# A state-space mixer: a block's weighted values move behind the whole gate, and the next transposes follow them

## The chip, the cores and the metric

The kernel runs on one core of a Trainium2 chip. The metric is the device time of one execution in microseconds (us), and a kernel's time is the median of its runs. Five engines matter here, each with its own queue of instructions that it works through in order: TensorE (PE; its weight loads are shown as PEld), VectorE (DVE), ScalarE (ACT), GpSimd (POOL) and SyncE (SP, which here only issues DMA transfers). Engines wait for each other on semaphores. An instruction that waits holds up everything behind it in its own queue.

## What is computed

The reference is one layer of a hybrid model over x of 4 x 256 tokens with 512 channels, in float32, four residual steps one after the other: attention, a feed-forward step with a choice of clusters, a state-space mixer, and the same feed-forward step again.

```python
x = x + attn(layernorm(x))
x = x + ffn(layernorm(x))
x = x + mixer(layernorm(x))     # the part that the change touches
x = x + ffn(layernorm(x))
```

The mixer projects 512 channels to a gate (8192), values (8192), B and C (1024 each) and a step dt (128), sends values, B and C through a causal convolution of four taps and SiLU, and then for each of 128 heads of 64 values:

```python
scores  = einsum('bcihn,bcjhn->bcijh', Cc, Bc) * Ldec * dt      # Ldec = exp(cum_i - cum_j), lower triangle
y_intra = einsum('bcijh,bcjhp->bcihp', scores, xc)
y       = y_intra + y_inter + D * x        # y_inter: the state carried over chunks of 32
g       = y * silu(gate)
out     = (g * rsqrt(mean(g*g per group of 1024) + eps) * norm_w) @ out_w.T
```

The kernel folds the carried state into the scores: for each head it holds the decay between pairs of 64-token pieces of a sequence of 256, so y is one weighted sum.

## The kernel before

The attention and the first feed-forward step take the first 22% of the time or so. The mixer then runs over 64 blocks of 128 channels, two heads each, and is what this document is about. Eight blocks form a group (g is the group, gi the block's place in it, 0 to 7), which shares one B and C and one normalization.

A block i, `block()` at L1514, has these pieces. The names are those of the tiles in the profile.

- **x**: the projection of its 128 value channels for all 1024 tokens, 24 matmuls of 128 x 512 (L115 to L117) in two halves of 12, into a PSUM tile `pp`. Each product is made of three matmuls on split operands. There are two `pp` buffers, and the projections of x, gate, B and C go through them in turn.
- **conv and taps**: ScalarE copies x with scale and bias (`acc`, L963), VectorE adds three taps (L973). ScalarE applies SiLU and writes the tile `x` (L1145), which needs a table load because the block also uses exp.
- **gate**: 24 more matmuls into the other `pp`, and SiLU on ScalarE into `gt` (L1436).
- **decays**: for two heads, VectorE subtracts cumulative steps (`em`, L1194 and L1195, `differences`), ScalarE takes exponentials (L1206 to L1214, `exponentials`, which begin with the exp table load), VectorE multiplies by the scores `gm` (L1219, `weighted`). There are three `em` buffers and two are used by a block. The differences are made at the end of block i, the exponentials and the product with `gm` in block i+1.
- **transposes**: `turned()` (L1221) sends x through eight 128 x 128 transposes on TensorE (`trx`, L1226) into two PSUM tiles, and VectorE multiplies both by dt into `xd` (L1229). There is one `xd` buffer.
- **weighted values**: `product()` (L1237) makes 64 small matmuls of `em` and `xd` into the PSUM tile `pyy` (L1245).
- **gating**: `gated()` (L1252) adds D times x (L1257, two instructions) and multiplies by `gt` (L1260) into `gb` on VectorE. `spilled()` (L1263) writes `gb` of block i-2 to DRAM. That DMA is issued from ScalarE's queue at the very start of block i, ahead of the block's exponentials. `squared()` (L1270) sums the squares on ScalarE and POOL.
- **output product**: at gi >= 2, and at gi = 0 from group 2 on, 24 matmuls (`pog`) for an eighth of an earlier group's output stand between x and gate. At gi = 1 the output product (`first_out`) stands after the gate instead, behind a sum of squares over the finished group (`pqs`, L1315), and `trq` (L1327) follows it. The first group has no output product. Its operands (`gh`, `wo`) are split into two parts on ScalarE (L1352, L1299) and VectorE (L1357, L1302), and so are the weights `w` (L910, L913).
- **B and C** of the next group are projected at the end of blocks gi = 3 and 4 and go through their own taps in the following block. Their scores (`pg`, L1163, `gm`, L1170) are made in block gi = 6; in group 0 the second half waits for block 7.

The tiles `tr`, `trx`, `pg`, `pog`, `pqs` and `trq` share one PSUM pool of two buffers (tag "m"), in the order in which they are made.

The order of the instructions on TensorE, VectorE, ScalarE and POOL is written out by hand in the mixer: they stand as the Python calls come. The values of block i-1 are thus finished in block i. Before the change, TensorE's order in a block with an output product is: first half of x(i), transposes of x(i-1), second half of x(i), output product, weighted values of i-1, gate(i). Without an output product between them it is: x(i) with the transposes of x(i-1) in its middle, gate(i), weighted values of i-1. `last_block()` (L1665) replaces the end of block 63.

Of the kernel before, what the change touches and what calls it, by code (L numbers as in the profile page):

```python
# [79 lines left out]
def hybrid_kernel(  # L80
# [789 lines left out]
    def mixer(feed, ps, mnorm, later):  # L870
        with ExitStack() as es, ExitStack() as inner:
# [32 lines left out]
            def upper_piece(i):  # L904

                if i >= NW:
                    return lambda: None
                w = pieces[i] = [pw.tile([P, KC, P], F32R, name=f"w{j}", tag=f"w{j}") for j in range(2)]
                r = raws.pop(i)
                nc.scalar.copy(w[0], r)  # L910

                def lower():
                    nc.vector.tensor_tensor(w[1], r, w[0].bitcast(F32), ALU.subtract)  # L913
                    fetch(i + 3)

                return lower
# [201 lines left out]
            def piece(v, j, c, k=0, n=None):  # L1118

                at, step = 4 * c + j * 7 + k * (1 + 2 * j), 1 + 2 * j  # L1120
                n = 4 - c - k if n is None else n
                return v[:, at : at + (n - 1) * step + 1 : step, :]
# [62 lines left out]
            def own_and_next(e):  # L1185
                return pieces_of(e, 0, 4, 4, 7), pieces_of(e, 1, 8, 2, 9)

            def differences(h):

                e = p2.tile([P, 20, Q], F32, name="em", tag="em", bufs=3)  # L1190
                own, next_ = own_and_next(e)
                rv = rr[h].rearrange("p (j c i) -> p j c i", j=2, c=4)
                cv = col_t[:, :, h : h + 1].rearrange("p (j c) h -> p j c h", j=2)
                nc.vector.tensor_tensor(own, rv, cv.to_broadcast([P, 2, 4, Q]), ALU.subtract)  # L1194
                nc.vector.tensor_tensor(  # L1195
                    next_, rv[:, :, 1::2, :], cv[:, :, 0::2].to_broadcast([P, 2, 2, Q]), ALU.subtract
                )
                return e
# [22 lines left out]
            def turned(n, x2):  # L1221

                xd = p2.tile([P, TT, P], F32, name="xd", tag="xd", bufs=1)
                trs = [ps.tile([P, 4, P], F32, name="trx", tag="m") for _ in range(2)]
                for c in range(TT):
                    nc.tensor.transpose(trs[c // 4][:, c % 4, :], x2[:, c * P : (c + 1) * P], ident)  # L1226
                for half, tr in enumerate(trs):
                    hs = slice(half * 4, half * 4 + 4)
                    nc.vector.tensor_tensor(  # L1229
                        xd[:, hs, :].rearrange("p c (h d) -> p c h d", h=2),  # L1230
                        tr.rearrange("p c (h d) -> p c h d", h=2),
                        dt_t[:, hs, 2 * n : 2 * n + 2].unsqueeze(3).to_broadcast([P, 4, 2, PD]),
                        ALU.mult,
                    )
                return xd

            def product(xd, es2):  # L1237
                py = ps_y.tile([P, 2, 2 * L], F32, name="pyy", tag="pyy")
                for j in range(2):
                    for c in range(4):  # L1240
                        for u in range(2):
                            us = slice(u * Q, (u + 1) * Q)
                            for hh in range(2):
                                d = slice(hh * PD, (hh + 1) * PD)
                                nc.tensor.matmul(  # L1245
                                    py[d, u, j * L + c * Q : (j + 1) * L].rearrange("p (k i) -> p k i", i=Q),
                                    xd[us, 4 * j + c, d], piece(es2[hh], j, c)[us],
                                    start=(c == 0), stop=(c == 3),
                                )
                return py  # L1250

            def gated(n, x2, gt, py):  # L1252

                gb = po_.tile([P, NT], F32, name="gb", tag="gb", bufs=3)
                for u, h in enumerate(hs):
                    k = lambda v: v.rearrange("p (k i) -> p k i", i=Q)
                    nc.vector.scalar_tensor_tensor(  # L1257
                        k(gb[:, h]), pair(x2)[:, :, u], dh[:, n : n + 1], k(py[:, u]), ALU.mult, ALU.add
                    )
                nc.vector.tensor_tensor(gb, gb, gt, ALU.mult)  # L1260
                return gb
# [124 lines left out]
            def projected(kind, n):  # L1386

                w = pieces.pop(at[kind, n])
                pp = (
                    ps_y.tile([P, NT], F32, name="pp", tag="pyy") if (kind, n) == ("g", 0)  # L1390
                    else ps_p.tile([P, NT], F32, name="pp", tag="pp")
                )
                for half in range(2):
                    yield pp
                    project(w, pp, slice(half * 512, half * 512 + 512))
                yield pp
# [27 lines left out]
            def outer(q, t):  # L1424

                po = ps.tile([P, C], F32, name="pog", tag="m")
                for half in range(2):
                    partial(po, q, parted.pop((q, 2 * t + half)), half)
                return q, t, po

            xs2, gts, ems, xds, gbs = {}, {}, {}, {}, {}
# [10 lines left out]
            def turn(i):  # L1442
                xds[i] = turned(i, xs2[i])
# [5 lines left out]
            def inner_products(i):  # L1449
                finish(i, product(xds.pop(i), ems.pop(i)))  # L1450

            def finish(i, py):
                gbs[i] = gated(i, xs2[i], gts.pop(i), py)
# [60 lines left out]
            def block(i):  # L1514
# [8 lines left out]
                def lowered():  # L1523
                    for f in lower:
                        f()
                    lower.clear()
# [20 lines left out]
                pp = next(x_steps)  # L1547
                waiting = [k for k in "bc" if k + "pp" in group]

                def begun_next(k):  # L1550
                    group[k] = conv(group[k + "pp"], (NB if k == "b" else NB + G) + g + 1, False)
# [11 lines left out]
                decays(i - 1, (0,) if between else (0, 1))  # L1563
                for k in waiting if g else ():
                    begun_next(k)
                turn(i - 1)
                if between:
                    weighted(ems[i - 1][0], gms[(i - 1) // GB])
                else:
# [14 lines left out]
                done = outer(*out) if out and not first_out else None  # L1584
# [6 lines left out]
                g_steps = projected("g", i)  # L1591
# [7 lines left out]
                both = i == NB - 1  # L1599
                scoring = None  # L1600

                def scored():
                    nonlocal scoring
                    if gi == 6 and g + 1 < G:
                        scoring = scores(group.pop("b"), group.pop("c"))
                        gms[g + 1] = next(scoring)
                        next(scoring)
                        next(scoring)

                next(g_steps)  # L1610
                for _ in pending:
                    for _ in pending.pop():
                        pass
                if done and not both:
                    inner_products(i - 1)
                    pp = next(g_steps)
                    scored()
                    next(g_steps)
                else:
                    pp = next(g_steps)  # L1620
                    next(g_steps)
                    scored()
                    if both:
                        return last_block(i, pp)
                    inner_products(i - 1)
                lower.append(upper_piece(n + 3))
                if g and gi == 0:
                    lower.append(upper_half(g - 1, 0))
# [1 line left out]
                if g and gi == 1:  # L1630
                    lower.append(upper_half(g - 1, 2))
                ems[i] = [differences(h) for h in (2 * i, 2 * i + 1)]
                lowered()
                if scoring and g:
                    for _ in scoring:
# [29 lines left out]
            def last_block(i, pp):  # L1665

                g = i // GB
                py = product(xds.pop(i - 1), ems.pop(i - 1))
                done = outer(G - 2, TT - 1)
                for k in range(3):  # L1670
                    fetch_out(NB - 3 + k)
                ems[i] = [differences(h) for h in (2 * i, 2 * i + 1)]
                made(0, 0)()
                gate(i, pp)
                decays(i, (0,))
                lower = [upper_out(g * GB + k) for k in range(4)]
                lower.append(made(1, 0))
                for f in lower[:2]:
                    f()
                scaled(*done)  # L1680
                for f in lower[2:]:
                    f()
                weighted(ems[i][0], gms[g])
                finish(i - 1, py)
                decays(i, (1,))
                made(2, 0)()
                turn(i)
                weighted(ems[i][1], gms[g])
                spilled(i - 1, gbs[i - 1])

            opening()
            for i in range(2, NB):
                block(i)
            es_p.close()
            ps_o = pool("m_o", 4, space=PSUM, **freed)
            i = NB - 1
# [208 lines left out]
```

## Time and profile before

| | |
|---|---|
| median of 3 runs | 1828.85 us (1825.78 to 1831.57) |
| the profiled execution, its own time | 1827.35 us |
| its span | 1825.5 us |
| mean granted clock of TensorE | 0.992 of full speed |
| PE busy | 1766.7 us |
| DVE busy | 1431.6 us |
| ACT busy | 1281.0 us |
| POOL busy | 249.8 us |
| a plain block of the mixer (start of pyy to start of pyy) | 19.8 us |
| a group of eight blocks | 173.1 us |

How to read the lines that follow. In a timeline a line gives the start (us from the span's start), the length, the engine, the line of the kernel, the operation, out<-in with sizes, the number of instructions merged, and in brackets the engine's idle time before it with what ended it. In the list of waits a line gives who waited for whom: us in total, times, the longest. In a table by stretches a line gives the stretch, its length, the busy time of PE, PEld, DVE, ACT and POOL (with instructions), the granted clock of TensorE, the DMA share and GB/s. In the page's first part a line gives the busy time of each engine with its share of the span. The chain is the work that ended last, followed back through what released each step.

### The profile page before, as it was taken

To read this page: it belongs to the slowest core of one execution; us is meant where nothing else is said; L and a number is where in the kernel's file an instruction comes from. 1 tells how busy PE (TensorE), PEld (TensorE's weight loads), DVE (VectorE), ACT (ScalarE), POOL (GpSimd) and SP (SyncE) were. 2 spreads that over 40 slices of the span, in tenths; PEclk is the share of its full clock that TensorE was granted. 3 is DMA by queue.
4 is the path that set the end of the run, shared out by engine and by line. 5 is a ranking of instruction groups with operands and counts; after the bars stand their busy time and mean duration, and the time that the engine had idled before them with its cause. 6 is when DMAs were issued, how large, how long until landed. Compare 5 with 4: busy or idle time off the path is not lost.

```text
span 1825.5 us, 33067 instructions
## 1 busy us (share of the span) xinstructions
PE 1766.7 (97%) x12862; PEld 1437.8 (79%) x12862; DVE 1431.6 (78%) x2163; ACT 1281.0 (70%) x2545; POOL 249.8 (14%) x255
## 2 busy tenths in 40 slices
PE   8999989899999999999999999999999999999998
PEld 6777767677877888888888888888888888888877
DVE  6566667788998788878878787879787878887777
ACT  6666676378788667766776686668667866777754
POOL 6322230010110111011101110010111011101100
PEclk9999999999999999999999999999999999999999
DMA  4000000212325323432442353325232533343231
GB/s 148 1 1 1 23 15 1 58 56 86 108 97 167 105 93 116 123 103 93 142 131 81 105 156 99 99 87 161 92 106 89 167 105 92 115 134 116 83 97 59
DMA packets 134381, 169.45 MB, mean 93 GB/s; under 512 B 12240, under 2 KB 77648, under 8 KB 134224
## 3 DMA queue, kind: packets, MB, share of 16 engines
q1 hardware_dynamic: 125152, 134.30, 24.5%
q10 hardware_dynamic: 9072, 33.03, 4.8%
q8 instruction: 101, 1.65, 0.4%
q14 instruction: 56, 0.46, 0.1%
HBM read 131.64 MB, written 35.65 MB: 92 GB/s over the span
## 4 chain that ended last, share of the span: by engine, by line
PE 81%; DVE 9%; ACT 6%; issue 2%; POOL 1%; DMA 1%; SPq 0%; ACTq 0%; DVEq 0%; POOLq 0%
PE pp L115 13%; PE pp L117 13%; PE pp L116 13%; PE pyy L1245 7%; PE pog L115 6%; PE pog L117 6%; PE pog L116 6%; PE trx L1226 3%; ACT e L504 2%; DVE acc L973 1%; PE pq L115 1%; PE ptr L520 1%; PE pq L116 1%; PE pq L117 1%; PE pg L1163 1%
## 5 line engine op out<-in xcount | busy, mean ns | idle before, releaser
L115 PE MATMUL pp<-mx,w 128*128 128x512 f32 x1144 | 459.6, 402 | 0.0
L117 PE MATMUL pp<-mx,w 128*128 128x512 f32 x1144 | 447.1, 391 | 0.0
L116 PE MATMUL pp<-mx,w 128*128 128x512 f32 x1144 | 446.5, 390 | 0.0
L1278 POOL TENSOR_TENSOR sq<-sq,x 128x1024 f32<-128x1024 f32 x54 | 132.1, 2447 | 1177.8 <-ACT x L1277 1177.8
L117 PEld LDWEIGHTS pp<-mx,w 128*128 128x128 f32 x1144 | 214.8, 188 | 46.0
L115 PEld LDWEIGHTS pp<-mx,w 128*128 128x128 f32 x1144 | 215.0, 188 | 44.6
L973 DVE SCALAR_TENSOR_TENSOR acc<-pp,cw_s,acc 128x1012 f32<-128x1012 f32 (+2 forms) x192 | 244.6, 1274 | 4.3
L116 PEld LDWEIGHTS pp<-mx,w 128*128 128x128 f32 x1144 | 215.3, 188 | 40.4
L1219 DVE TENSOR_TENSOR em<-em,gm 128x1280 f32<-128x1280 f32 x128 | 189.6, 1489 | 72.1 <-ACT em L1214 72.0
L115 PE MATMUL pog<-wo,gh 128*128 128x512 f32 x512 | 201.3, 393 | 1.9 <-DVE x L1374 1.9
L117 PE MATMUL pog<-wo,gh 128*128 128x512 f32 x512 | 200.3, 391 | 0.9 <-DVE gh L1357 0.9
L116 PE MATMUL pog<-wo,gh 128*128 128x512 f32 x512 | 200.0, 391 | 0.0
L1229 DVE TENSOR_TENSOR xd<-trx,dt_t 128x512 f32<-128x512 f32 x128 | 82.4, 686 | 141.4 <-PE trx L1226 141.4
L1145 ACT ACT_TABLE_LOAD x63 | 80.8, 1283 | 138.8 <-DVE acc L973 138.7
L1436 ACT ACTIVATE gt<-pp 128x1024 f32<-128x1024 f32 x64 | 65.7, 1026 | 145.3 <-PE pp L117 145.3
L1245 PEld LDWEIGHTS pyy<-em,xd 64*64 64x64 f32 x4096 | 130.3, 133 | 44.1 <-issue 17.3
L1206 ACT ACTIVATE em<-r,end_t 128x128 f32<-128x128 f32 x512 | 163.0, 389 | 0.8
L1245 PE MATMUL pyy<-em,xd 64*64 64x256 f32 (+3 forms) x4096 | 157.8, 300 | 3.1 <-DVE em L1219 2.9
L504 ACT ACTIVATE e<-sc,nmx 128x256 f32<-128x256 f32 (+1 forms) x256 | 104.0, 441 | 21.0 <-DVE nmx L498 20.9
L115 PEld LDWEIGHTS pog<-wo,gh 128*128 128x128 f32 x512 | 96.3, 188 | 24.7 <-issue 2.7
L117 PEld LDWEIGHTS pog<-wo,gh 128*128 128x128 f32 x512 | 96.4, 188 | 22.3 <-DVE gh L1357 2.1
L116 PEld LDWEIGHTS pog<-wo,gh 128*128 128x128 f32 x512 | 96.5, 188 | 19.4
(327 smaller groups left out, 3191.9 us busy)
## 6 DMA issues: line engine op xcount, KB each, us to landing
wr<-in_win_dram SPq DMA_DIRECT2D x144, 256.0 KB, 2.7
r<-cumd SPq DMA_DIRECT2D x256, 128.0 KB, 2.9
spill<-gb ACTq DMA_DIRECT2D x63, 512.0 KB, 2.8
gr<-spill SPq DMA_DIRECT2D x120, 256.0 KB, 3.4
wor<-in_wout_dram SPq DMA_DIRECT2D x64, 256.0 KB, 4.7
out_dram<-x SPq DMA_DIRECT2D x7, 256.0 KB, 2.9
x<-in_x_dram SPq DMA_DIRECT2D x1, 1536.0 KB, 8.8
gr<-spill SPq DMA_DIRECT2D x8, 192.0 KB, 2.5
```

The source lines that it names most:

```text
L115: nc.tensor.matmul(o, lh, rh, start=(first and k == 0), stop=False)
L116: nc.tensor.matmul(o, lh, rl, start=False, stop=False)
L117: nc.tensor.matmul(o, ll, rh, start=False, stop=(last and k == n - 1))
L504: nc.scalar.activation(es_[c][:, 2 * j + pr, :], sc[:, j, :], AF.Exp, bias=nm[:, j : j + 1], accum_out=rs[:, c, h : h + 1],)
L973: nc.vector.scalar_tensor_tensor(av[:, :, d:], pv[:, :, : L - d], cw_s[:, ch, tap : tap + 1], av[:, :, d:], ALU.mult, ALU.add,)
L1145: nc.scalar.activation(pair(x2).rearrange("p k u i -> p u k i"), acc.rearrange("p (u k i) -> p u k i", u=2, i=Q), AF.Silu,)
L1206: nc.scalar.activation(piece(e, j, c, 2 - c, 2), rv[:, j, 2:, :], AF.Exp, bias=end_t[:, 2 * j + c, h : h + 1],)
L1219: nc.vector.tensor_tensor(e, e, gm, ALU.mult)
L1229: nc.vector.tensor_tensor(xd[:, hs, :].rearrange("p c (h d) -> p c h d", h=2), tr.rearrange("p c (h d) -> p c h d", h=2), dt_t[:, hs, 2 * ...
L1245: nc.tensor.matmul(py[d, u, j * L + c * Q : (j + 1) * L].rearrange("p (k i) -> p k i", i=Q), xd[us, 4 * j + c, d], piece(es2[hh], j, c)[us ...
L1278: (nc.gpsimd if n < NB - 2 else nc.vector).tensor_tensor(sqs[g], sqs[g], x2, ALU.add)
L1436: nc.scalar.activation(gts[i], pp, AF.Silu)
```

## The change

No instruction is added or removed. In every block from 2 on:

- the weighted values of block i-1 always go behind both halves of gate(i), as they did before only where there was no output product;
- the transposes of x(i), with their two VectorE products, are issued in block i itself, directly behind these weighted values, instead of in the middle of x(i+1) in the next block. Block 2 still turns x(1) at the old place, since the opening does not;
- the gating of block i-1 (`finish`) is issued after those transposes. On VectorE the order at the end of a block becomes: `em` differences of i, `xd` of i, `gb` of i-1, then the subtractions that were collected in `lower`. Before it was `gb`, `em`, the subtractions, and `xd` in the next block.

On SP and POOL the order stays the same. On ScalarE too the instructions keep their order.

```diff
@@ block(i), between the two halves of x(i) @@
                 decays(i - 1, (0,) if between else (0, 1))
                 for k in waiting if g else ():
                     begun_next(k)
-                turn(i - 1)
+                if i == 2:
+                    turn(i - 1)
                 if between:
                     weighted(ems[i - 1][0], gms[(i - 1) // GB])
                 else:
@@ block(i), from the gate on @@
-                if done and not both:
-                    inner_products(i - 1)
-                    pp = next(g_steps)
-                    scored()
-                    next(g_steps)
-                else:
-                    pp = next(g_steps)
-                    next(g_steps)
-                    scored()
-                    if both:
-                        return last_block(i, pp)
-                    inner_products(i - 1)
+                pp = next(g_steps)
+                next(g_steps)
+                scored()
+                if both:
+                    return last_block(i, pp)
+                py = product(xds.pop(i - 1), ems.pop(i - 1))
                 lower.append(upper_piece(n + 3))
                 ...
                 ems[i] = [differences(h) for h in (2 * i, 2 * i + 1)]
+                turn(i)
+                finish(i - 1, py)
                 lowered()
```

`inner_products(i)` was `finish(i, product(...))`, so `product` and `finish` are the same calls as before, now apart.

## The prediction

> **What bounds the kernel now.** I read the page's busy shares and chain first, then the waits, then the timelines of single blocks.
>
> ```profile
> PE 1766.7 (97%) x12862; PEld 1437.8 (79%) x12862; DVE 1431.6 (78%) x2163; ACT 1281.0 (70%) x2545; POOL 249.8 (14%) x255
> ...
> PE 81%; DVE 9%; ACT 6%; issue 2%; POOL 1%; DMA 1%; SPq 0%; ACTq 0%; DVEq 0%; POOLq 0%
> ```
>
> TensorE is the bound. The list of waits shows how far behind it the others are:
>
> ```profile
> ACT gt L1436 <- PE pp L117: 145.3, 47, 5.2
> DVE xd L1229 <- PE trx L1226: 141.4, 48, 6.3
> ACT L1145 <- DVE acc L973: 138.7, 54, 4.9
> DVE em L1219 <- ACT em L1214: 72.0, 83, 1.2
> ```
>
> VectorE waits about 3 us a block for the transposes, ScalarE 3 us for the gate: that is all the slack there is. One plain block (gi=0) on ScalarE, then on VectorE; its transposes started at 1048.40:
>
> ```profile
> 1045.94 0.33 ACTq L1266 DMA_DIRECT2D spill<-gb  x1
> 1046.91 1.28 ACT L1206 ACT_TABLE_LOAD   x1
> 1060.35 1.06 ACT L1145 ACTIVATE x<-acc 128x1024 f32<-128x1024 f32 x1
> ...
> 1049.04 1.29 DVE L1229 TENSOR_TENSOR xd<-trx,dt_t 128x512 f32<-128x512 f32 x2 [3.57 <-PE trx L1226]
> 1055.08 3.89 DVE L973 SCALAR_TENSOR_TENSOR acc<-pp,cw_s,acc 128x1012 f32<-128x1012 f32 x3
> 1060.15 1.40 DVE L1257 SCALAR_TENSOR_TENSOR gb<-x,dh,pyy 128x512 f32<-128x512 f32 x2
> ```
>
> The new x is ready at 1061.41, 14.50 after the exp table load; today nobody asks for it until the next block. The second block of a group (gi=1), which has no output product between x and gate, on TensorE, VectorE, ScalarE:
>
> ```profile
> 1077.34 2.41 PE L1245 MATMUL pyy<-em,xd 64*64 64x256 f32 x64
> 1079.68 0.64 PE L1315 MATMUL pqs<-sq,ones 128*32 128x256 f32 x8
> ...
> 1079.89 2.73 DVE L1302 SCALAR_TENSOR_TENSOR wo<-wor,nw_s,wo 128x512 fp32r<-128x512 f32 x4
> 1082.54 1.40 DVE L1257 SCALAR_TENSOR_TENSOR gb<-x,dh,pyy 128x512 f32<-128x512 f32 x2
> ...
> 1080.66 1.06 ACT L1145 ACTIVATE x<-acc 128x1024 f32<-128x1024 f32 x1
> ```
>
> Here x ends at 1081.72, 2 us after pyy has left TensorE, and VectorE is late too. Two waits that will matter exist already, in the first group and in the last block:
>
> ```profile
> 441.74 0.33 ACTq L1266 DMA_DIRECT2D spill<-gb  x1
> 442.15 1.28 ACT L1206 ACT_TABLE_LOAD   x1 [1.91 <-DVE gb L1260]
> ...
> 1724.25 0.69 DVE L1194 TENSOR_TENSOR em<-r,col_t 128x512 f32<-128x512 f32 x1 [3.67 <-PE pyy L1245]
> ```
>
> The spill sits on ScalarE's queue ahead of the exponentials, so they wait for gb. The second em tile of a block waits for pyy of the block before, since there are three em buffers.
>
> **The change: what is removed.** No instruction. Per block 64 pyy matmuls move behind 24 gate matmuls, and 8 transposes (L1226) plus their 2 VectorE products xd (L1229) move from inside the next x to directly behind pyy, ahead of gb. None of them issues a DMA. The order on SP and POOL stays; only the spill's issue on ScalarE is met later, because its gb is later. Going back from float32 to the projection's matmuls costs 0.10 (1017.34 to 1017.67, against 0.227 a matmul). pyy and trx now share one return: between 0 and 0.2 a block saved; I take 0.1, as measured for one return. A plain block has 19.78 now (pyy at 1098.16 and 1117.94), so TensorE would need 19.68: 16.31 for 72 matmuls, 2.44 for pyy with the 0.10 of lead-in that it shows (1014.68 to 1015.00), 0.89 for the transposes and the return (1048.40 on), and 0.04 of small gaps.
>
> **What is added: a loop.** Call T the start of a block's transposes, X that of xd. pyy ends 0.07 after T, em's second tile starts 0.08 later and takes 0.94 (1724.25 to 1725.19): X = T+1.09. xd 1.21 (1029.24 to 1030.45), gb 2.66 (1060.15 to 1062.81), then 0.43 to the table load: X+4.30. x follows at +14.50, with 0.05 for the signal: the next T is at least T + 1.09 + 4.30 + 14.50 + 0.05 = T+19.9. Before, the load followed the gate 1.5 us before the transposes; now it comes 5.4 behind them. VectorE closes a loop of its own, since xd stands behind the scaled output, the weight and gh subtractions and em: 4.30 + 11.98 (load to end of taps, 1058.89) + 2.46 (1119.22 to 1121.68) + 1.87 (1104.34 to 1106.21) = 20.6. What is queued behind the waiting spill is all of a block's exponentials, then the copy that opens the taps; behind the waiting xd it is gb, and so the spill again. Both loops are longer than 19.68.
>
> **Group by group**, with gi the block's place in its group of eight (a group takes 173.1 us now, pyy at 1015.06 and 1188.18):
> - gi=3 and gi=0: 19.9 each instead of 19.8, +0.3 together. In gi=3 VectorE's loop is the longer (20.6 from X to X, where T moves 18.85 from X), so it ends 1.8 behind: X = T+1.8.
> - gi=4: the 5.44 us b projection gives the x loop room, but VectorE's b taps end at X + 4.30 + 8.17 (load to taps, 1055.08) + 3.82 (three taps, 461.04 to 464.86), 18.1 after T, and the gate wants their PSUM buffer at 0.89 + 16.31 = 17.2 (0.89 is the transposes with their return): a stall of 0.9, less 0.1 saved: +0.8. gi=5, with X = T+1.1 again: +0.1.
> - gi=6 and 7: scores and transposes share two PSUM buffers. VectorE does the first gm products (0.92) and em (1.87) before xd, so X = T+1.4. The third score tile waits for half of xd (0.69), at T+2.1 instead of T+0.9, the fourth for the rest; x starts at T+3.45. T to T: 21.3 in gi=6 (0.89 + 16.31 + two score tiles with a wait for the scaled output, 1.65, + 2.44), 3.45 + 16.31 + 2.44 = 22.2 in gi=7, together 43.5 against 42.6: +0.9.
> - gi=1: TensorE reaches the transposes at 0.89 + 10.88 + 2.44 = 14.2 after T of gi=0. x is ready at 1.09 + 4.30 + 15.01 (load 1066.71, x 1081.72; ScalarE's wo copies delay it by 0.5) = 20.4. VectorE then has wo and em to finish: X = 1.09 + 4.30 + 15.83 (to 1082.54) + 1.87 = 23.1. pqs and pog need the two PSUM buffers that xd frees, so pog starts at 24.5 instead of 15.6, a stall of 8.9. gi=1 and gi=2 together: 48.9 against 40.5 (pyy at 1057.62 and 1098.16): +8.4. In gi=2 ScalarE's chain has 3 us to spare, so TensorE does not get it back and does not lose more.
> - The clock, once a group behind gi=1's stall. The nearest row is the stall at 1754, with the clock in the third column from the right:
>
> ```profile
> 1754.00:1756.00 2.00, 0.07 (x2) 0.07 (x1) 1.86 (x5) 0.10 (x1) 0.00 (x0) 1.00 0.56 168
> 1756.00:1758.00 2.00, 2.00 (x8) 1.58 (x9) 1.57 (x6) 0.90 (x3) 0.00 (x0) 0.83 0.77 258
> 1758.00:1760.00 2.00, 2.00 (x6) 1.46 (x5) 1.93 (x5) 0.00 (x0) 0.00 (x0) 0.50 0.06 17
> ```
>
> TensorE idled 1.93; from 1757.19 to 1760.05 seven matmuls took 2.86 where 1.59 is usual, the transposes behind them 0.3 too long: 1.6 lost. Bounds: 0 (if gi=1's transposes keep it awake) and 3.2 (two dips); I take 1.6, the row itself.
>
> The Trainium skill, "TensorE: Matmul & The Clock Gate", Part 1, says that the clock halves after an idle window of about 3.4 us and needs about 3.4 us of work to return. That speaks against this change: it would price a dip at 1.7, in all 7 x 1.7 = 12 where the row gives 7 x 1.6 = 11. The row shows that a shorter idle can do it.
>
> A group thus costs 0.3 + 0.8 + 0.1 + 0.9 + 8.4 + 1.6 = 12.1 more. From gi=2 of group 1 to gi=2 of group 7 there are six: **+73**.
>
> **First group**, where VectorE and ScalarE already lead and there is no output product: load to x is 13.1 (529.84 to 542.95), so a block is 1.09 + 4.30 + 13.1 = 18.5 against 15.1 to 16.4. The two blocks with b and c taps take 21.0 (b is done 6.5 after T, its copy and the load 7.7, x 13.3 later), the two behind scores 19.35 (gm 0.92 more ahead of xd). Blocks 3 to 8: 2 x 18.5 + 2 x 21.0 + 2 x 19.35 = 117.7, against 102.9 (pyy ended at 438.95 in block 2, at 541.9 in block 8): **+15**. Group 1's gi=1 and 2: 48.9 + 1.6 against 39.2: **+11**. **Tail**: group 7 has four plain blocks at VectorE's 20.6, +3; the last block's exponentials come 2 later: **+5**.
>
> **Sum**: 15 + 11 + 73 + 5 = 104. The profiled execution took 1827.35 (span 1825.5), 1.5 under the median of 1828.85, inside the runs' spread. **1931 us**.
>
> **The rivals.**
> - *Faster.* TensorE stays the bound everywhere, 62 x 0.1 saved: 1821. For it: 97% busy. It needs x ready when pyy ends; gi=1's rows are 2 us on the wrong side even with nothing moved. It would decide if the x loop were under 19.68 and gi=1's under 14.2.
> - *No loop.* gb later does not hold the exponentials (the spill finds gb done). Then gi=1 alone stalls: VectorE reaches xd at 1082.54 + 1.87 = 1084.4 and ends it 1.29 later, pog starts at 1085.8 instead of 1081.1 (pyy's end, 0.79 for the transposes, 0.57 for pqs): 7 x (4.7 + 1.6) = 44, less 6 saved: 1865. It decides where gb ends 5 us sooner than I put it. Against it: the 1.91 wait at 442.15.
> - *Plain blocks pay as well.* If a pass of the loop has 1 us more than the rows say (VectorE's weight subtraction, 0.69 alone, takes 1.67 at 508.02), some 45 blocks without other slack lose it: 1976. Against it: every row of the loop comes from blocks with the same neighbours. It decides from 0.1 us on, since 19.9 is already over 19.8.
>
> **How the numbers follow.** About 0.3% is what a measurement can tell. My forecast 0.76 (own range 1900 to 1960), no loop 0.10, plain blocks too 0.11, faster 0.03. The range 1864 to 1966 leaves out the faster case, half of the no-loop case and half of the upper one, and a little of my own. Faster 0.03, same 0.01, slower 0.96.
>
> **What would show it.** TensorE's busy share falls to some 92 to 94%, with waits of trx for x (ScalarE L1145) near 6 us in gi=1 and pqs or pog for xd; exp table loads wait for gb in nearly every block; the wait of xd for trx shrinks from 141; the clock dips once a group. It is wrong if the loads start before gb ends, or if gi=1's pog follows pyy within 3 us.

## The result, and the profile after

The change makes the kernel slower: the median is 1936.01 us (1932.91 to 1938.68, four runs) against 1828.70 us for the kernel before on the same chip (1825.78 to 1831.57, four runs). The ratio is 1.0586, with a 95% interval of 1.0563 to 1.0610. The profiled execution has a span of 1933.5 us, 108.0 more than the 1825.5 before.

The page of the kernel after: busy shares, the granted clock in 40 slices of the span, and the chain that ended last.

```profile
PE 1797.8 (93%) x12862; PEld 1456.8 (75%) x12862; DVE 1431.6 (74%) x2163; ACT 1274.8 (66%) x2545; POOL 249.6 (13%) x255
...
PEclk9999999999999998999999989999999899999999
...
PE 49%; DVE 27%; ACT 15%; issue 5%; DMA 2%; POOL 1%; ACTq 1%; SPq 0%; DVEq 0%; POOLq 0%
```

The instructions are the same 12862, 2163, 2545 and 255 as before, VectorE is busy as long as before, and ScalarE 6 us less. TensorE's share falls from 97% to 93%. The line that matters most is the chain: TensorE held 81% of it, and now holds 49%, with VectorE at 27% and ScalarE at 15%. The work that sets the end now runs round all three engines.

The list of waits of the kernel after (who waited for whom: us in total, times, the longest):

```profile
DVE em L1219 <- ACT em L1214: 258.0, 117, 3.9
ACT L1206 <- DVE gb L1260: 242.3, 52, 6.6
ACT L1145 <- DVE acc L973: 135.3, 54, 4.5
...
PEld trx L1226 <- ACT x L1145: 40.0, 27, 4.1
...
DVE em L1194 <- PE pyy L1245: 37.3, 33, 2.2
...
PE trx L1226 <- ACT x L1145: 35.0, 14, 4.0
```

ScalarE's wait for `gb` was in the list of before too, but small:

```profile
ACT L1206 <- DVE gb L1260: 10.3, 4, 5.1
```

Two waits of before are gone: ScalarE's for the gate (`gt`, 145.3 us) is down to 2.0, and VectorE's `xd` no longer waits for the transposes (141.4, now 0.5 by the view of the tile `trx`). Their time did not become free. ScalarE now waits 242.3 us ahead of its exponential table load (L1206) for `gb`, in 52 blocks, and VectorE waits 258.0 us for the exponentials that are late for it (72.0 before). TensorE, whose transposes had never waited for x, now waits for it.

One pass of the loop, from the transposes of gi=7 to those of gi=0 (a plain block), as the timelines of VectorE, ScalarE and TensorE show it. The transposes `trx` started at 1096.12, so T = 1096.12.

```profile
1097.19 1.28 DVE L1229 TENSOR_TENSOR xd<-trx,dt_t 128x512 f32<-128x512 f32 x2
1098.39 1.40 DVE L1257 SCALAR_TENSOR_TENSOR gb<-x,dh,pyy 128x512 f32<-128x512 f32 x2
1099.82 1.23 DVE L1260 TENSOR_TENSOR gb<-gb,gt 128x1024 f32<-128x1024 f32 x1
...
1101.08 0.33 ACTq L1266 DMA_DIRECT2D spill<-gb  x1
1101.49 1.28 ACT L1206 ACT_TABLE_LOAD   x1 [6.02 <-DVE gb L1260]
...
1114.93 1.06 ACT L1145 ACTIVATE x<-acc 128x1024 f32<-128x1024 f32 x1
...
1116.04 1.09 PE L1226 MATMUL trx<-con,x 128*128 128x128 f32 x8
```

`xd` starts at T+1.07, the table load 4.30 behind it, and the next transposes 14.55 behind the load: 19.92 from T to T. ScalarE stood idle for 6.02 us with the exponentials queued behind a DMA issue. x ends at 1115.99, 0.05 ahead of the transposes, which reach their place at about the same time. So TensorE hardly shows a wait here, though the pass sets the block's length.

The worst place, gi=1 of the same group, on TensorE and then on VectorE and ScalarE:

```profile
1129.54 2.40 PE L1245 MATMUL pyy<-em,xd 64*64 64x256 f32 x62 [0.93 <-DVE em L1219]
1135.92 1.97 PE L1226 MATMUL trx<-con,x 128*128 128x128 f32 x8 [3.97 <-ACT x L1145]
1139.77 1.08 PE L1315 MATMUL pqs<-sq,ones 128*32 128x256 f32 x8 [1.89 <-DVE xd L1229]
1140.78 0.80 PE L115 MATMUL pog<-wo,gh 128*128 128x512 f32 x1
...
1134.42 2.73 DVE L1302 SCALAR_TENSOR_TENSOR wo<-wor,nw_s,wo 128x512 fp32r<-128x512 f32 x4
1138.94 1.29 DVE L1229 TENSOR_TENSOR xd<-trx,dt_t 128x512 f32<-128x512 f32 x2
...
1134.81 1.06 ACT L1145 ACTIVATE x<-acc 128x1024 f32<-128x1024 f32 x1
```

The transposes wait 3.97 us for x, which ScalarE ends at 1135.87. Then `pqs` waits for `xd`, and VectorE is late with `xd` because four `wo` subtractions and the differences stand ahead of it. The output product `pog` starts 24.7 behind the T of 1116.04.

The same place in the table by stretches (third column from the right: the granted clock of TensorE):

```profile
1131.00:1135.00 4.00, 0.95 (x31) 0.81 (x22) 3.96 (x5) 3.97 (x7) 1.52 (x1) 0.99 0.07 23
1135.00:1139.00 4.00, 1.97 (x8) 1.57 (x8) 4.00 (x9) 2.81 (x4) 0.00 (x0) 0.50 0.84 245
1139.00:1143.00 4.00, 3.23 (x13) 2.06 (x14) 3.97 (x7) 1.66 (x2) 0.00 (x0) 0.50 0.39 148
1143.00:1147.00 4.00, 4.00 (x14) 3.14 (x13) 1.00 (x2) 0.00 (x0) 0.00 (x0) 0.73 0.45 131
```

The clock is granted in full until the stall and by half behind it, well into `pog`. The page's clock row shows such a dip as an 8 in three of its slices, in groups 2, 4 and 6. In the other four groups it does not show in that row, but the clock is 0.50 behind the stall there too (952 to 956 in group 3), and `pqs` takes 1.08 us in all seven groups and 0.64 in the kernel before.

### The profile page after: what moved, and what is told of

Read it like the earlier page. It is cut to its first block, busy times and chain, and to the rows that moved or that the text cites. A ratio compares the mean times of both kernels' runs of the same rounds, so it can differ in the third digit from the quotient of the medians.

```text
span 1933.5 us, 33054 instructions
## 1 busy us (share of the span) xinstructions
PE 1797.8 (93%) x12862; PEld 1456.8 (75%) x12862; DVE 1431.6 (74%) x2163; ACT 1274.8 (66%) x2545; POOL 249.6 (13%) x255
## 3 DMA queue, kind: packets, MB, share of 16 engines
q1 hardware_dynamic: 125152, 134.30, 22.5%
## 4 chain that ended last, share of the span: by engine, by line
PE 49%; DVE 27%; ACT 15%; issue 5%; DMA 2%; POOL 1%; ACTq 1%; SPq 0%; DVEq 0%; POOLq 0%
PE pp L115 7%; PE pp L116 7%; PE pp L117 7%; ACT em L1206 4%; PE pyy L1245 4%; PE pog L115 4%; PE pog L116 4%; PE pog L117 4%; DVE acc L973 3%; DVE xd L1229 3%; DVE em L1219 3%; DVE gb L1257 2%; DVE em L1194 2%; ACT L1206 2%; DVE gb L1260 2%
## 5 line engine op out<-in xcount | busy, mean ns | idle before, releaser
L1219 DVE TENSOR_TENSOR em<-em,gm 128x1280 f32<-128x1280 f32 x128 | 190.9, 1492 | 258.1 <-ACT em L1214 258.0
L1206 ACT ACT_TABLE_LOAD x64 | 82.1, 1283 | 243.6 <-DVE gb L1260 242.3
L115 PE MATMUL pog<-wo,gh 128*128 128x512 f32 x512 | 207.0, 404 | 1.9 <-DVE x L1374 1.9
L117 PE MATMUL pog<-wo,gh 128*128 128x512 f32 x512 | 203.6, 398 | 0.5 <-DVE gh L1357 0.5
L116 PE MATMUL pog<-wo,gh 128*128 128x512 f32 x512 | 204.0, 398 | 0.0
L1245 PE MATMUL pyy<-em,xd 64*64 64x192 f32 (+3 forms) x4096 | 165.7, 304 | 15.5 <-DVE em L1219 15.3
L1245 PEld LDWEIGHTS pyy<-em,xd 64*64 64x64 f32 x4096 | 135.3, 135 | 57.7 <-DVE em L1219 22.4
L1206 ACT ACTIVATE em<-r,end_t 128x128 f32<-128x128 f32 x512 | 163.1, 389 | 0.8
L115 PEld LDWEIGHTS pog<-wo,gh 128*128 128x128 f32 x512 | 99.3, 194 | 28.5 <-DVE xd L1229 5.7
L1194 DVE TENSOR_TENSOR em<-r,col_t 128x512 f32<-128x512 f32 x128 | 89.2, 697 | 38.0 <-PE pyy L1245 37.3
L117 PEld LDWEIGHTS pog<-wo,gh 128*128 128x128 f32 x512 | 99.1, 194 | 22.4 <-DVE gh L1357 0.9
L1226 PE MATMUL trx<-con,x 128*128 128x128 f32 x512 | 76.1, 295 | 42.3 <-ACT x L1145 35.0
```

The costliest lines, as they stand in the source:

```text
L115: nc.tensor.matmul(o, lh, rh, start=(first and k == 0), stop=False)
L116: nc.tensor.matmul(o, lh, rl, start=False, stop=False)
L117: nc.tensor.matmul(o, ll, rh, start=False, stop=(last and k == n - 1))
L1206: nc.scalar.activation(piece(e, j, c, 2 - c, 2), rv[:, j, 2:, :], AF.Exp, bias=end_t[:, 2 * j + c, h : h + 1],)
L1219: nc.vector.tensor_tensor(e, e, gm, ALU.mult)
L1245: nc.tensor.matmul(py[d, u, j * L + c * Q : (j + 1) * L].rearrange("p (k i) -> p k i", i=Q), xd[us, 4 * j + c, d], piece(es2[hh], j, c)[us ...
```

## The experiments

The theory: two things cost the time. One is a loop from the transposes over `xd`, `gb`, the spill's issue on ScalarE's queue, the exponentials and x back to the transposes. The other is gi=1, where no output product gives x time, and where the late x costs a stall and then the clock. The rivals were that one half of the change alone does the damage (late values, or early transposes), that the loop has more to it than the spill, and that the half clock only accompanies the stall.

Each kernel's time stands beside the kernel before on the same chip (1830.35, 1828.51 or 1829.33 us, medians of 7 to 17 runs). "After" stands for the changed kernel, whose 1936 us the numbers are compared with.

### The values alone

The kernel before, with the weighted values always behind the gate, and the transposes where they were:

```diff
-                if done and not both:
-                    inner_products(i - 1)
-                    pp = next(g_steps)
-                    scored()
-                    next(g_steps)
-                else:
-                    ...
+                pp = next(g_steps)
+                next(g_steps)
+                scored()
+                ...
+                inner_products(i - 1)
```

> The kernel before, with one half of the change: the weighted values always behind the gate, the transposes in their old place in the next x, gb directly behind the weighted values. Theory (the loop is closed only by transposes that need x and stand ahead of gb): 1828 us, 1824 to 1834, because gb still ends 3 us behind pyy and the x of a block has a whole half projection more time. Rival (weighted values behind the gate make gb, and so the exponentials, late whatever the transposes do): 1860 and over.

Measured: 1860.35 us, ratio 1.0164 (1.0148 to 1.0181). The theory's number was missed and the rival's met. Yet the reason is not that late exponentials slow every block. The list of waits of this kernel:

```profile
ACT L1206 <- DVE gb L1260: 173.9, 51, 5.1
...
PE trx L1226 <- DVE x L1374: 16.8, 8, 2.2
...
PE trx L1226 <- DVE gm L1170: 11.8, 7, 1.8
```

The exponentials wait for `gb` in 51 blocks, and plain blocks still take 19.8 us and the blocks with B and C 25.2, as before: with the transposes a block later, x has the room. The loss sits in the blocks whose transposes need a PSUM buffer that VectorE now frees later. From transposes to transposes it is 24.2 in place of 22.8 in gi=6 to 7 (the scores `gm`), and 21.2 + 22.2 to 23.8 in place of 20.6 + 19.9 in gi=0 to 2 (the scaled output, L1374). The timeline of TensorE there:

```profile
1105.38 1.12 PE L1226 MATMUL trx<-con,x 128*128 128x128 f32 x4 [2.19 <-DVE x L1374]
```

The second half of the transposes waits 2.19 us, and the granted clock is 0.50 from 1106 to 1108. The same wait, 2.2 us, stands in all six steady groups, but half clock followed it in two of them alone (groups 3 and 4, those with 23.7 and 23.8). So `gb` ahead of the gate had also kept VectorE's queue clear for the pool of two buffers.

### The transposes alone

The changed kernel, with values and `gb` ahead of the gate again where an output product stands there:

```diff
-                pp = next(g_steps)
-                next(g_steps)
-                scored()
-                if both:
-                    return last_block(i, pp)
-                py = product(xds.pop(i - 1), ems.pop(i - 1))
+                early = done and not both
+                if early:
+                    inner_products(i - 1)
+                    pp = next(g_steps)
+                    scored()
+                    next(g_steps)
+                else:
+                    ...
...
-                finish(i - 1, py)
+                if not early:
+                    finish(i - 1, py)
```

> The changed kernel with the other half alone: where a block has an output product, the weighted values and gb stand ahead of the gate again as before, and only the transposes are at the end of the block. Theory: the loop is open in blocks with an output product (gb is done long before the spill), so plain blocks take 19.7, but the first group (no output product) and gi=1 stay as in the change: 1890 us (1875 to 1905). Rival (the loop through gb is worth nothing, all is the place of the transposes): 1936. Rival (the transposes are harmless without the late gb): 1830.

Measured: 1895.69 us, ratio 1.0357 (1.0332 to 1.0382), as expected. The line of its list of waits that carries the theory:

```profile
ACT L1206 <- DVE gb L1260: 22.4, 6, 5.1
```

The wait for `gb` is left in six places, plain blocks take 19.8 us and the B and C blocks 25.2, but gi=1 and gi=2 still take 46 to 48 us in place of 40.5, and the first group's blocks are nearly as long as in the changed kernel (117.8 us for blocks 3 to 8, there 118.5), since they have no early values anyway. The halves alone cost 30 and 65 us (1860.35 and 1895.69 less 1830.35). Their sum, 95, is less than the 107 of both.

### The spill on another queue

The changed kernel, with the spill's DMA issued from SP and not from ScalarE. This takes ScalarE's queue out of the loop; the same write now stands in SP's queue.

```diff
-                    nc.scalar.dma_start(spill[(n // GB) % 2][n % GB], gb)
+                    load(spill[(n // GB) % 2][n % GB], gb)
```

> The changed kernel, with the spill of gb issued from SP instead of ScalarE. Nothing else moves. Theory (the late gb holds the spill, the spill holds the block's exponentials, and they hold the next x): about 1885 us (1870 to 1900), since the exp table loads then follow the gate again, plain blocks return to 19.7, the first group loses its 18.5 us blocks, and gi=1 keeps most of its stall because VectorE's own queue (gb, the wo and gh subtractions, em, then xd) is still late there. The waits of the exp table load for gb, 242 us now, go to nearly nothing. Rival (only the place of the transposes in gi=1 costs; the spill is hidden anyway): 1936, unchanged.

Measured: 1883.92 us, ratio 1.0299 (1.0279 to 1.0319), 52 less than the changed kernel, as expected. On ScalarE's timeline the table load has no wait ahead of it:

```profile
1068.46 1.28 ACT L1206 ACT_TABLE_LOAD   x1
```

Its wait for `gb` is gone from the list. What stands in the list of waits in its place:

```profile
DVE em L1194 <- PE pyy L1245: 179.9, 48, 5.5
...
PEld trx L1226 <- ACT x L1145: 46.0, 12, 6.2
PE trx L1226 <- ACT x L1145: 44.3, 11, 6.1
```

VectorE now has slack again (it waits for `pyy` to free an `em` buffer, 4.30 us in one plain block). Plain blocks take 19.75, the B and C blocks 25.2 as before, and the first group is back to 15.7 and 21.1 a block. A steady group takes 181.0 us, 5.0 less than in the changed kernel but 7.9 more than before. Of the gain, 30 us lie in the six steady groups, 13 in the first group and 9 behind the last gi=2.

What is left is in gi=1, where the transposes still wait up to 6.1 us for x. The expectation gave VectorE's late queue as the reason. ScalarE's timeline there (T = 1089.40) shows a second one:

```profile
1104.37 0.62 ACT L1352 CAST gh<-gr 128x512 fp32r<-128x512 f32 x1 [5.67 <-DMA gr<-spill]
```

`gh` is made from `gr`, which is the spilled `gb` read back from DRAM, and x stands behind it on ScalarE. The waits for this read are 40.6 us in 9 places here, 5.2 in 5 in the kernel before, and 3.7 in 2 in the changed kernel, where ScalarE comes to `gh` later. VectorE's taps end at 1104.78; with the table load (1.28) and SiLU (1.06) directly behind them x would end near 1107.2, and it ends at 1109.82. So, by an estimate from these rows, VectorE's queue makes 3.5 of the 6.1 and the read 2.6. The late `gb` thus holds up x by a second way, over DRAM and back, which the prediction does not have.

### The transposes of gi=1 where they were

```diff
-                if i == 2:
+                if gi == 2:
                     turn(i - 1)
...
-                turn(i)
+                if gi != 1:
+                    turn(i)
```

> The changed kernel with one block in eight undone: in gi=1 the transposes stand in the next x again. Theory: the stall of 8.9 us and its cold clock go, some 2 us of it come back as a wait of the next output product for xd: 7 groups x 8 = 57 less, 1880 us (1868 to 1892). Rival (the loss is spread over all blocks by the loop, gi=1 only shows it): 1920 and over.

Measured: 1892.04 us, ratio 1.0338 (1.0322 to 1.0353): 44 less than the changed kernel, where 57 were expected, at the very edge of the range. gi=1 and gi=2 together take 44.4 in place of 50.4 to 51.4, but not the 40.5 of before. The list of waits names one part of the rest:

```profile
PEld trx L1226 <- DVE x L1374: 17.3, 8, 5.0
PE trx L1226 <- DVE x L1374: 15.4, 8, 4.8
```

The moved transposes meet the late scaled output, as in the run with the values alone: 1.5 us in gi=2 of each group (the 4.8 is in the last block). The other waits of TensorE in these two blocks are 0.9 for `em` ahead of `pyy`, whose exponentials still come late, and 0.6 for the squares ahead of `pqs`.

### What VectorE's queue costs in gi=1

The changed kernel, with the four `wo` subtractions of gi=1 behind `xd` and `gb` and not ahead of them:

```diff
-                    lower.extend(upper_out((g - 1) * GB + k) for k in range(4, 8))
+                    held = [upper_out((g - 1) * GB + k) for k in range(4, 8)]
...
                 turn(i)
                 finish(i - 1, py)
+                if g and gi == 1:
+                    for f in held:
+                        f()
```

> The changed kernel, with the four wo subtractions of gi=1 (2.65 us of VectorE) behind xd instead of ahead of em and xd. Theory (the last 4.5 us of the gi=1 stall are VectorE's queue ahead of xd, which holds the two PSUM buffers that pqs and pog need): xd comes some 2.6 us earlier, up to where x itself is the limit, 7 x 2.3 = 16 less, 1920 us (1914 to 1926). Rival (pqs waits for x and the transposes alone): 1936.

Measured: 1918.88 us, ratio 1.0493 (1.0477 to 1.0509), as expected. TensorE's timeline in gi=1:

```profile
1130.97 1.97 PE L1226 MATMUL trx<-con,x 128*128 128x128 f32 x8 [3.97 <-ACT x L1145]
1132.96 1.08 PE L1315 MATMUL pqs<-sq,ones 128*32 128x256 f32 x8
```

The wait for x is the same 3.97 us, but `pqs` follows directly. So 17 us of what the stall costs are VectorE's queue, separate from the late x.

### The clock

Two kernels put idle float32 matmuls (ones by columns of the residual x) around gi=1's transposes, to keep TensorE awake in the stall. Their sums go to PSUM tiles that the next real matmuls overwrite; they add work and change no output. The first had eight ahead and six behind:

```diff
                 trs = [ps.tile([P, 4, P], F32, name="trx", tag="m") for _ in range(2)]
+                warmed(trs[0].rearrange("p a b -> p (a b)"), [x[:, 0, :]] * busy)
...
-                turn(i)
+                if g and first_out:
+                    turn(i, 8)
+                    warmed(ps_p.tile([P, NT], F32, name="pp", tag="pp"), [x[:, 0, :]] * 6)
+                else:
+                    turn(i)
```

> The changed kernel with 14 idle matmuls a group added in gi=1 (ones by x, 8 ahead of the transposes, 6 behind them), which write PSUM that is written again before it is read. They do not shorten any wait. Theory (TensorE's clock halves in the stall, and the sum of squares and the output product behind it pay for it): pqs takes half as long and the output product 5.6 us instead of 6.5 to 7.6, so 7 groups x 2 less, about 1922 us (1918 to 1928). Rival (the clock is not the cause, the output product waits for something else): 1936 or more.

Measured: 1959.13 us, ratio 1.0711 (1.0695 to 1.0727), slower than the changed kernel, and undecided: each of these matmuls is two instructions and takes 0.87 us (6.97 from the first of the eight to the transposes), so eight outlasted the stall. TensorE's timeline:

```profile
1142.24 7.13 PE L122 MATMUL trx<-x,ones 128*128 128x512 f32 x16
1149.21 1.04 PE L1227 MATMUL trx<-con,x 128*128 128x128 f32 x8
...
1155.33 0.64 PE L1316 MATMUL pqs<-sq,ones 128*32 128x256 f32 x8
```

`pqs` at 0.64 shows that the clock was kept, but the transposes came later. The second had `turn(i, 4)` and `* 3`, sized to fit into the stall:

> After, with 4 idle f32 matmuls (two instructions of 0.43 us each, 0.87 together by the run with 8 and 6, so 3.5 us in all) between group 1's gi=1 values and its transposes, and 3 of them (2.6 us) behind the transposes, ahead of pqs; their sums go to a PSUM tile that the next real matmuls overwrite, so they add work and change no output. They fit into the stall of 3.97 us that the transposes have there anyway. If the half clock behind the stall is a cost of its own: pqs near 0.6 us in place of 1.08, and pog to trq 5.6 us in place of 7.64 and 6.58 in turn, so 2.0 us per group less, times 7: about 1922 us (1917 to 1928). If the half clock is only a sign of the stall and costs nothing more: 1936 us, and if the idle matmuls delay the transposes, above that.

Measured: 1922.59 us, ratio 1.0514 (1.0493 to 1.0535), 13.4 less than the changed kernel, with more work in it. TensorE's timeline:

```profile
1127.74 3.70 PE L122 MATMUL trx<-x,ones 128*128 128x512 f32 x8
1131.78 1.09 PE L1227 MATMUL trx<-con,x 128*128 128x128 f32 x8 [0.34 <-ACT x L1145]
1132.71 2.74 PE L122 MATMUL pp<-x,ones 128*128 128x512 f32 x6
1135.63 0.64 PE L1316 MATMUL pqs<-sq,ones 128*32 128x256 f32 x8 [0.18 <-DVE xd L1230]
1136.20 0.50 PE L115 MATMUL pog<-wo,gh 128*128 128x512 f32 x1
...
1141.82 0.38 PE L1328 MATMUL trq<-con,rows__11906 128*128 128x128 f32 x2
```

The output product takes 5.62 from `pog` to `trq`, where it took 7.6 and 6.5 to 6.6 in turn in the changed kernel, and the granted clock stays at 1.00 throughout. The half clock is thus a cost of its own: 13.4 / 7 = 1.9 us a group.

### Both causes taken away

The spill on SP and gi=1's transposes at the old place, the two edits above together:

> Both of the edits of the first call on the changed kernel: the spill on SP, and the transposes of gi=1 back in the next x. Theory (the loop through the spill and the stall of gi=1 are the two causes, and what stays is the wait of the transposes in gi=2 for the late scaled output that holds their PSUM buffer, 2 to 4 us a group with its cold clock, and the scores in gi=6): 1846 us (1838 to 1854). If both were independent and complete, 1936 - 52 - 44 = 1840. Rival (a third cause of the same size): 1870 and over.

Measured: 1846.96 us, ratio 1.0094 (1.0074 to 1.0113), as expected in the number: 89 of the 107 us are gone, near the sum of the two edits alone (52 + 44 = 96). A steady group takes 175.3 us, 2.2 more than before. What stays is not what was expected, though. In the steady groups the transposes no longer wait for the scaled output. TensorE waits in gi=1 ahead of `trq`, and ScalarE, 8 us earlier, for the read of the spilled `gb`:

```profile
1094.11 0.44 PE L1327 MATMUL trq<-con,rows__11861 128*128 128x128 f32 x2 [2.00 <-ACT rows__11861 L1320]
...
1086.39 0.62 ACT L1352 CAST gh<-gr 128x512 fp32r<-128x512 f32 x1 [5.59 <-DMA gr<-spill]
```

`trq` needs a copy of the sums (L1320) that stands on ScalarE behind `gh`, `wo`, x and the gate. It waits 1.7 to 2.0 us for it in each of the six steady groups, at a granted clock of 1.00. That is nearly all of the 2.2.

### The spill on SP in the kernel before

```diff
-                    nc.scalar.dma_start(spill[(n // GB) % 2][n % GB], gb)
+                    load(spill[(n // GB) % 2][n % GB], gb)
```

> The kernel before, with the spill of gb issued from SP. Theory: in the first group, and only there, ScalarE waits 1.7 to 2 us a block for gb at the spill; without it blocks of 15.1 to 16.4 come down to some 14.6, five to six of them, 5 to 8 us less: 1823 us, ratio 0.996. From the second group on nothing changes, since gb is done before the gate. Rival (VectorE's own queue is the limit in the first group): 1829, ratio 1.000.

Measured: 1825.92 us, ratio 0.9979 (0.9970 to 0.9988), about half of the expected gain and inside 0.3%. It lies in the first group, as expected (100.5 us for six blocks in place of 102.8), and a steady group takes 173.1 as before. In the kernel before, the spill on ScalarE cost next to nothing; the 52 us that it costs in the changed kernel come from the change. This is the fastest kernel of the study, by a margin too small to recommend it on.

## Why the prediction was right

The forecast was 1931 us, 5 under the result, and its account held in nearly every term. The parts are read from T to T in the profile of after, as the prediction read them:

| part | predicted | measured |
|---|---|---|
| before block 3 | 0 | +1.0 |
| first group, blocks 3 to 8 | 117.7, +15 | 118.5, +15.6 |
| group 1's gi=1 and gi=2 | 50.5, +11 | 20.0 + 30.4 = 50.4, +11.2 |
| six steady groups | 12.1 each, +73 | 186.04 less 173.11 = 12.9 each, +77.6 |
| tail | +5 | what is left of 108.0: +2.6 |
| sum | 104 | 108.0 |

The 1.0 before block 3 is not the change's: the mixer's first transposes, ahead of everything that was moved, already start 1.0 later (417.66 against 416.64). The tail was priced too high: only three of group 7's plain blocks take 20.6 and the one at gi=3 takes 19.9, which makes 2.6, and the 2 us put on the last block's exponentials do not show in the sum; the reason was not traced. So there is some luck in the 4 us between the sums: the steady groups were put 4.6 too low, and the tail 2.4 too high.

Within a steady group:

| blocks | before | predicted | measured |
|---|---|---|---|
| gi=3, gi=0 | 19.8 | 19.9 each | 19.9 each |
| gi=4 | 25.2 | 26.0 | 26.2 |
| gi=5 | 25.2 | 25.3 | 25.6 |
| gi=6 and 7 | 42.6 | 43.5 | 21.0 + 22.5 = 43.5 |
| gi=1 and 2, with the clock | 40.5 | 48.9 + 1.6 = 50.5 | 50.4 and 51.4 in turn |

**The loop.** Its terms were put at 1.09, 4.30 and 14.55; the trace has 1.07, 4.30 and 14.55. That the spill is what closes it is shown by moving that one DMA: 52 us. VectorE's own loop of 20.6 is there too, in the three plain blocks gi=4 to 6 of group 7 (20.6 each).

**gi=4.** The stall at the b taps was put at 0.9. On TensorE's timeline of after:

```profile
1019.09 0.47 PE L115 MATMUL pp<-mx,w 128*128 128x512 f32 x1 [0.85 <-DVE bc L973]
```

gi=5 was under-priced at +0.1. Its b taps end 17.4 behind T (1044.48 less 1027.05), the gate wants their buffer at 17.2, and its first weight load starts at 17.5 (1044.59): the same stall again, 0.3 long. The prediction's terms for gi=4 would have shown it. The last 0.2 of gi=4 was not traced.

**The saving.** It was put at 0.1 a block for the values and transposes sharing one return to the projection's matmuls. Where nothing else limits a block, with the spill on SP, a plain block takes 19.75 where it took 19.79 before: 0.04, inside the stated 0 to 0.2. The 0.06 that are missing lengthen only the blocks that TensorE sets, gi=4 and gi=5 among them.

**gi=1.** x was put at 20.4 behind T and came at 19.8; `xd` at 23.1 and came at 22.9; `pog` at 24.5 and came at 24.7. The waits of the transposes for x are 4.0, not near 6, because x comes 0.6 earlier than put and TensorE gets there 1.7 later, 15.9 behind T (1131.94) in place of 14.2: `pyy` itself is late, since it waits 0.93 for `em` behind its first two matmuls. The prediction did not see this, and it costs nothing since x is later still. The 24.7 instead of 24.5 is the half clock in `pqs`, which takes 1.08.

**The clock.** The 1.6 taken from one row measured 1.9, from the run that keeps TensorE awake. The changed kernel's own rows give the same: 0.44 in `pqs`, and 2.0 or 1.0 in the output product. The Trainium skill, "TensorE: Matmul & The Clock Gate", Part 1, says that the clock halves after an idle window of about 3.4 us, that it returns after as long a time of work, and that the window runs freely, so that the place of the return varies. The trace agrees with the first in gi=1 (3.97 idle, then 0.50). Elsewhere it does not: 0.50 also followed waits of 1.93 (the prediction's row) and 2.19 (the values alone), and there the measurement decides. An alternating cost, and a dip behind some of the waits of 2.2 only, would fit a free window, but no run here shows the window itself. By an estimate from the page's 3.4 us, that time at half speed would cost 1.7.

**The rivals.** "Faster" fell with the loop. "No loop" (1865) failed at its own condition: the loads do wait for `gb`, 52 times. "Plain blocks pay as well" (1976) failed too, since a pass is 19.9 long as its rows said.

Of the signs that were named, the busy share, the waits of the loads, the vanished wait of `xd` and the dip of the clock in every group are all there. The one that is off is the size of the wait for x in gi=1.

**What stays open.** The kernel with both causes taken away is still 18 us over the kernel before (its profiled execution, the fastest of its four, 14). Some 13 of it are the 2.2 us of each steady group, most of it in gi=1 and gi=2 (42.5 against 40.5), where the trace shows ScalarE's queue held by the read of the spilled `gb`. No run takes that wait away, so its price is read from the trace and not shown by an edit. Nor was it tried how much of it SP's queue adds: the read is issued 9.7 behind T there, and 9.1 in the changed kernel.

## What to carry to other kernels

When work is moved later on one engine, follow what its late result holds up in every in-order queue, DMA issues on a compute engine's queue above all: here a write to DRAM that was nearly free in the old order cost 52 us in the new one, because exponentials stood behind it. Add up one full pass round the engines, and compare it with the block time of the bound engine, not with the waits that the profile shows: 3 us of waits on the other engines were no slack once the pass was 19.9 against 19.7. And price the place without filler by itself: gi=1 with the block behind it held 10.4 of a group's 12.9 us.

## What the runs showed of the hardware

- Behind the same stall the half clock lasted for a different part of the output product: in the changed kernel `pog` to `trq` took 7.6 us in groups 2, 4 and 6 and 6.5 to 6.6 in the four others, against 5.58 in the kernel before. The wait for x was 3.97 in all seven. The same stall thus cost one or two us in the output product; what decides which is not shown.
- A wait of 2.2 us on TensorE was followed by half clock in two of six groups of the run with the values alone, and one of 1.7 to 2.0 in none of six in the run without both causes.
- Filling a stall with idle work made the kernel faster (13.4 us for 7 places). The same trick with twice the work made it 23 us slower, since a float32 matmul of 128 x 512 takes 0.87 us, nearly four times the 0.227 of one of the projection's.
- Bringing the values and the transposes together saved 0.04 us a block, where one return to the projection's matmuls showed 0.10.
